# Padded score products, spread scans and row maxima split on GpSimd in a four-layer kernel

## The chip, the cores and the metric

The kernel runs on one core of a Trainium2 chip, as one launch. The metric is the device time of that core in microseconds: 1718.79 us as the median of three runs (1716.07 to 1720.85). An engine is named as the profile names it: PE is TensorE (matmuls), PEld its weight loads, DVE is VectorE, ACT is ScalarE, POOL is GpSimd, SP is SyncE, which issues the DMAs.

## The reference

The input is x of shape (4, 1024, 128), float32. Four layers follow one another, each as `x = x + layernorm(layer(layernorm(x)))`:

- a time-mixing layer: a recurrence over the 1024 positions with maxima and exponentials, then a feed-forward part of width 512,
- 16 gated experts of width 64 (4 of them chosen for each token) and a shared one,
- linear attention with 16 heads of 8: two decays for each head, and for every position a state that is multiplied by the decay and increased by key times value; the result is (query times state) / (query times summed keys),
- softmax attention and 8 experts (2 chosen). This last layer is the one that the change touches most:

```python
attn = jnp.einsum('bqhd,bkhd->bhqk', q, k) * scale
attn = jnp.where(causal, attn, -inf)
attn = jax.nn.softmax(attn, axis=-1)
out = jnp.einsum('bhqk,bkhd->bqhd', attn, v).reshape(B, S, C)
h = x + out @ wo.T
out = h + _moe(_rmsnorm(h, ffn_norm_w), gate_w, expert_w)
```

with S = 1024, 16 query heads of 8 dimensions, and 4 key heads, each used by 4 query heads.

## The kernel before

**Stages.** x is held transposed, 128 channels on the partitions, 512 positions (a half, `h`) in a tile. The time-mixing layer (`stage_a`) runs for three of the four batch items side by side. Then come the experts (`gates_b`, `stage_b`) with the linear attention of items 0 and 1 (`stage_c`) and the preparation of attention for item 0 (`heads`, `spread`). Up to here a scheduler orders the instructions of each engine. From `with tc.manual_schedule()` on, the order is the one in which the program issues them: this is the attention stage. It holds the attention of all four items, the linear attention of items 2 and 3, `heads` of items 1 to 3, and the last experts.

**Linear attention.** In `stage_c` the two states of a head and value dimension e are scans along the 512 positions on VectorE (`scan`, L620): one scan for each of two decays and nine e (eight value dimensions and the key sum), so 18 scans for a half. GpSimd makes key times value (`keyed`, L614) and adds the two states (`add`, L631), VectorE multiplies by the query (`times_q`, L637), TensorE sums over heads (`num_ps`, L674). Each bare `yield` ends a step.

**Attention.** float32 scores are made out of bfloat16 products: a query is split into three bfloat16 parts and so is a key, and the nine pairs of parts times eight dimensions are 72 contraction rows. Queries of a half lie in a tile `qr` of 128 partitions, 16 heads and 512 positions, keys in `keys_r`; `spread` fills rows 0 to 71 of both by DMA (L849, L853). Three more rows hold the row maximum, in three bfloat16 parts, against key rows that are -1: so the product of 75 rows (`KROWS` = 72, `ROWS` = 75) is the score less its maximum, and ScalarE takes the exponential straight from it.

For a block (b, i) of 128 queries there are two kinds of unit:

- `maxima(b, i)`: scores of 72 rows (`sm`; `late` at L874 for the half that the block lies in, with a causal mask added at L878, and `early` at L886 for the first half), and a maximum on VectorE for each (L882, L887). The last unit, `rows`, splits the maxima into three bfloat16 parts: five small VectorE instructions on 16 columns (L894 to L898; L894 only for blocks of the second half). The transpose on TensorE (`m_ps`, L901) is issued 9 ticks later, its copy (L905) 1 tick after that, and the three DMAs that place the rows in `qr` (L909) 3 ticks after that.
- `weighted(b, i)`: the 75-row product `sc` (L945), its exponential `pr` on ScalarE (L950), a causal select on GpSimd for the diagonal (L954), and, seven units later, the product with the values `av` (L937).

`units_of` interleaves the units of `weighted` for block n with those of `maxima` for block n + 2.

**Order in the attention stage.** After each unit the program calls `tick`. A tick issues what has come due, one step of `spread` if one is under way, and, by two accounts, steps of other work: `owed[0]` grows by `PER_TICK` = 0.5 and pays for one step of `front` (the linear attention and `heads` of the later items) whenever it has reached 1.0; `owed[1]` grows by 0.65 and pays for a step of the last experts (`experts`, `behind_it`). So the front advances one step in two ticks. Before block (b, 0) and block (b, 5) the program needs `heads` of (b, 1) and (b + 1, 0); if they are not ready, it calls `advance` until they are, with no unit in between:

```python
if i == 5 and b + 1 < NB:
    while (b + 1, 0) not in ready:
        advance()
```

Each engine takes its instructions in the order of issue, so an instruction that waits holds up those behind it on its engine.

Of the kernel before, what the change touches and what calls it, by code (L numbers as in the profile page):

```python
# [11 lines left out]
FP = mybir.dt.float32  # L12
BF = mybir.dt.bfloat16
AF = mybir.ActivationFunctionType
ALU = mybir.AluOpType
AX = mybir.AxisListType
PSUM = bass.MemoryType.PSUM

P = 128
NB = 4  # L20
T = 1024
CH = 512
NH = T // CH
# [16 lines left out]
def sandwich(ctx: ExitStack, tc: tile.TileContext, x, vecs, cmats, rope, wa, wb, wc, wd, out):  # L40
# [3 lines left out]
    nc = tc.nc  # L44
# [471 lines left out]
    rope3 = rope.rearrange("p (a t) -> p a t", a=2)  # L516

    LAG = 8

    def wait_for_it():  # L520
        for _ in range(LAG):
# [11 lines left out]
    def stage_c(b, pp, banks=None):  # L533
# [14 lines left out]
        for h in range(NH):  # L548
# [55 lines left out]
            q, k = phi  # L604
# [37 lines left out]
            for n, e in enumerate(order + [None, None, None]):  # L642

                if n + 1 < len(order):
                    keyed(order[n + 1])
                if e is not None:
                    scan(e, 0)
                    yield
                    scan(e, 1)
                    if 0 <= e < 5:  # L650
                        fetch(e + 3)
                yield
                if 1 <= n <= len(order):
                    add(order[n - 1])
                yield
                if 2 <= n <= len(order) + 1:
                    times_q(order[n - 2])
                yield
                if n == 3:
                    den = pp([P, CH], "den_ps")  # L660
                    parts = sums_e.pop(8)
                    for m, s_ in enumerate(parts):
                        nc.tensor.matmul(den, lhsT=selden, rhs=s_, start=(m == 0), stop=(m == len(parts) - 1))
                    yield
                    qz = pc.tile([P, CH], FP, tag="qz", name="qz", bufs=1)
                    nc.scalar.activation(qz, den, AF.Ln, bias=eps6)
                    nc.scalar.activation(qz, qz, AF.Exp, scale=-1.0)
                if n in ((7, 11) if banks is None else (6, 10)):
                    part = n // 8
                    pn = pp([P, CH], "num_ps")  # L670
                    four = [sums_e.pop(4 * part + e4) for e4 in range(4)]
                    for m in range(len(four[0])):
                        for e4 in range(4):
                            nc.tensor.matmul(  # L674
                                pn[32 * e4 : 32 * e4 + 32, :], lhsT=into[:, part, :], rhs=four[e4][m],
                                start=(m == 0), stop=(m == len(four[0]) - 1),
                            )
                    yield
                    o = pc.tile([P, CH], FP, tag="o", name="o")
                    nc.vector.tensor_mul(o, pn, qz)  # L680
                    os.append(o)
# [42 lines left out]
    while running or waiting:  # L724
        if waiting and (len(running) == 0 or (len(running) < SIDE and count >= BEHIND)):
            b = waiting.pop(0)
# [41 lines left out]

    KROWS, ROWS = 72, 75
    keys_r = [pk.tile([P, NH, 4, CH], BF, name=f"keys_r{i}") for i in range(2)]
    for kr in keys_r:
        nc.gpsimd.memset(kr[64:128], -1.0)

    def parts3(dst, src):

# [1 line left out]
        nc.gpsimd.tensor_copy(dst[:, 1], src)  # L779
        nc.gpsimd.tensor_sub(dst[:, 2], src, dst[:, 1])  # L780

    n3s, qrs, vas, drams, sums, pavs = {}, {}, {}, {}, {}, {}
    held = deque()
    behind_it = deque()
    moving = deque()


    now, due = [0], []
# [52 lines left out]
    def spread(b, h):  # L841

        dq, dk = drams[b]
        kr = keys_r[b % 2]
        qr = qrs[b, h] = pe.tile([P, 16, CH], BF, tag="qr", name="qr")
        for i in range(3):
            for j in range(3):
                rows = slice(3 * i + j, KROWS, 9)
                nc.sync.dma_start(  # L849
                    out=kr[rows, h].rearrange("r g t -> r (g t)"),  # L850
                    in_=dk[h, j].rearrange("(d g) t -> d (g t)", d=8),
                )
                nc.sync.dma_start(  # L853
                    out=qr[rows].rearrange("r h t -> r (h t)"),
                    in_=dq[h, i].rearrange("(d h) t -> d (h t)", d=8),
                )
                yield

    def maxima(b, i):


        qr, kr = qrs[b, i // 4], keys_r[b % 2]
        tb = slice(i % 4 * P, (i % 4 + 1) * P)
        half = i // 4
        n_s = (i % 4 + 1) * P
        in_bank = CH // n_s
        ms = pe.tile([P, 2, 16], FP, tag="ms", name="ms", bufs=3)

        def late(h0):
            sc = to_max([P, CH], "sm")  # L870
            view = r3(sc[:, : in_bank * n_s], in_bank)
            for k in range(in_bank):
                h = h0 + k
                nc.tensor.matmul(  # L874
                    view[:, k, :], lhsT=qr[0:KROWS, h, tb], rhs=kr[0:KROWS, half, h // 4, 0:n_s],
                    start=(k == 0), stop=False, skip_group_check=True,
                )
            nc.tensor.matmul(  # L878
                view[:, :, n_s - P :], lhsT=identb, rhs=later[:, :in_bank, :], start=False, stop=True,
                skip_group_check=True,  # L880
            )
            nc.vector.tensor_reduce(ms[:, 0, h0 : h0 + in_bank], view, AX.X, ALU.max)  # L882

        def early(h):
            sc = to_max([P, CH], "sm")
            nc.tensor.matmul(sc, lhsT=qr[0:KROWS, h, tb], rhs=kr[0:KROWS, 0, h // 4, :], start=True, stop=True)  # L886
            nc.vector.tensor_reduce(ms[:, 1, h : h + 1], sc, AX.X, ALU.max)  # L887

        def rows():
            mp = pe.tile([P, 3, 16], BF, tag="mp", name="mp", bufs=3)  # L890
            left = pe.tile([P, 16], FP, tag="ml", name="ml", bufs=3)
            top = ms[:, 0]
            if half:
                nc.vector.tensor_max(top, top, ms[:, 1])  # L894
            nc.vector.tensor_copy(mp[:, 0], top)
            nc.vector.tensor_sub(left, top, mp[:, 0])
            nc.vector.tensor_copy(mp[:, 1], left)
            nc.vector.tensor_sub(mp[:, 2], left, mp[:, 1])  # L898
            def turned():
                pm = to_max([48, P], "m_ps", BF)  # L900
                nc.tensor.transpose(pm, mp.rearrange("p i h -> p (i h)"), identb)  # L901

                def kept():
                    mt = pe.tile([48, P], BF, tag="mt", name="mt", bufs=3)
                    nc.vector.tensor_copy(mt, pm)  # L905

                    def placed():
                        for k in range(3):
                            nc.sync.dma_start(  # L909
                                out=qr[KROWS + k : KROWS + k + 1, :, tb], in_=mt[16 * k : 16 * k + 16, :]  # L910
                            )
                        placed_rows.add((b, i))

                    later_on(3, placed)

                later_on(1, kept)

            later_on(9, turned)

        units = [lambda h0=h0: late(h0) for h0 in range(0, 16, in_bank)]  # L920
        if half:
            units += [lambda h=h: early(h) for h in range(16)]
        return units + [rows]

    def weighted(b, i):


        qr, kr, va = qrs[b, i // 4], keys_r[b % 2], vas[b]
        tb = slice(i % 4 * P, (i % 4 + 1) * P)

        def products():
# [170 lines left out]
    def units_of(n):  # L1102

        first = weighted(*blocks[n])
        second = []
        if n + AHEAD < len(blocks):
            b, i = blocks[n + AHEAD]
            assert (b, i // 4) in qrs
            while moving:
                whole(moving.popleft())  # L1110
            second = maxima(b, i)
        done = 0
        for k, u in enumerate(first):
            yield u
            while done < len(second) and (done + 1) * len(first) <= (k + 1) * len(second):
                yield second[done]
                done += 1
        yield from second[done:]
# [13 lines left out]
    coming = front()  # L1132
    PER_TICK, PER_TICK_BEHIND = 0.5, 0.65
    owed = [0.0, 0.0]

    def advance():
        if next(coming, True):
            owed[0] = -1.0e9

    def tick():  # L1140
        now[0] += 1
        while due and min(due, key=lambda d: d[0])[0] <= now[0]:
            first = min(due, key=lambda d: d[0])
            due.remove(first)
            first[1]()
        if moving and next(moving[0], True):
            moving.popleft()
        owed[0] += PER_TICK
        if owed[0] >= 1.0:
            owed[0] -= 1.0  # L1150
            advance()
        owed[1] = min(owed[1] + PER_TICK_BEHIND, 1.5)
        if behind_it and owed[1] >= 1.0:
            owed[1] -= 1.0
            if next(behind_it[0], True):
                behind_it.popleft()
# [122 lines left out]
```

## Time and profile before

The profiled execution took 1715.55 us; its span from the first to the last instruction is 1713.8 us. The mean granted clock of TensorE is 0.85 of full speed. Where the stages lie, by the first and last records of their tiles:

| part | from, us | to, us |
|---|---|---|
| experts (`y_ps`) with linear attention of items 0 and 1 | 221 | 706 |
| scans of the linear attention, item 2, two halves | 826, 965 | 883, 1021 |
| scans of the linear attention, item 3, two halves | 1147, 1290 | 1216, 1356 |
| attention, first maximum of the manual order to last `sc` | 736 | 1659 |
| last experts after the attention | 1660 | 1714 |

The largest groups of the attention stage and those that the change touches:

| instruction | count | busy, us | mean, ns |
|---|---|---|---|
| ACT exponential `pr`, L950 | 576 | 328.2 | 595 |
| PE `sc`, 75 rows x 512, L945 | 576 | 234.1 | 422 |
| DVE maximum over 512, `early`, L887 | 256 | 165.0 | 682 |
| PE `sm`, 72 rows x 512, `early`, L886 | 256 | 99.6 | 417 |
| DVE scan with carried state, L620 | 32 | 49.8 | 1559 |
| POOL key times value, L614, attention stage | 35 | 48.6 | 1393 |

Busy times of one engine may be added up; those of different engines lie beside each other. [...]

### The profile page before, as it was taken

Reading aid. Unit: us, or ns where it says so; the run is one execution under the profiler, and the core shown is the slowest. Engines: PE = TensorE matmul, PEld = TensorE weight load, DVE = VectorE, ACT = ScalarE, POOL = GpSimd, SP = SyncE. Lnnn points to the kernel's source line nnn. Section 1 sums busy time; section 2 is a strip of 40 time slices with the busy share of each in tenths; the row PEclk is TensorE's granted clock in tenths of the full one; section 3 lists DMA queues with packets and bytes.
Section 4 is the critical chain, followed back from the end, with each engine's and each line's share of the span. In section 5 each row is a group of like instructions: output and inputs, shape, how many; then the busy total and the mean of one; then the engine's idle time right before and its main releaser. Section 6 shows DMA issues by size and latency. Waiting matters only on the chain.

```text
span 1713.8 us, 15167 instructions
## 1 busy us (share of the span) xinstructions
PE 1310.6 (76%) x4593; PEld 463.3 (27%) x4604; DVE 1168.9 (68%) x1991; ACT 856.7 (50%) x1565; POOL 655.9 (38%) x663
## 2 busy tenths in 40 slices
PE   2547887867865889678779869888887879889864
PEld 1213333312221323133223223322232223233311
DVE  4575676698775877867995597777779825577601
ACT  3457776624453457234436625645553345645561
POOL 5554353524252324323433363427227333122212
PEclk8669998978887999877779869987898669989996
DMA  2000110313033122101112111231113011110101
GB/s 97 13 7 6 25 50 25 96 40 108 13 111 110 53 65 85 44 12 34 45 58 70 53 57 54 70 92 46 38 37 101 21 48 64 45 61 29 54 22 56
DMA packets 59330, 90.49 MB, mean 53 GB/s; under 512 B 9904, under 2 KB 26800, under 8 KB 58544
## 3 DMA queue, kind: packets, MB, share of 16 engines
q1 hardware_dynamic: 59248, 89.52, 17.3%
q8 instruction: 36, 0.59, 0.1%
q14 instruction: 46, 0.38, 0.1%
HBM read 76.38 MB, written 12.71 MB: 52 GB/s over the span
## 4 chain that ended last, share of the span: by engine, by line
PE 32%; DVE 18%; ACT 6%; issue 4%; POOL 4%; DMA 2%; SPq 0%; POOLq 0%; DVEq 0%; ACTq 0%
PE av L937 8%; PE sc L945 5%; DVE ms L882 4%; DVE st L620 4%; ACT pr L950 3%; PE sm L874 3%; DVE ms L887 3%; PE y L1074 3%; PE sm L886 2%; PE ln_v L138 2%; PE num_ps L674 1%; POOL hid L473 1%; POOL share L1062 1%; PE sm L878 1%; PE g_ps L138 1%
## 5 line engine op out<-in xcount | busy, mean ns | idle before, releaser
L950 ACT ACTIVATE pr<-sc 128x512 f32<-128x512 f32 x576 | 328.2, 595 | 361.7 <-PE sc L945 358.0
L882 DVE TENSOR_REDUCE ms<-sm 128x1 f32<-128x512 f32 (+3 forms) x352 | 210.5, 633 | 114.2 <-PE sm L878 103.0
L945 PE MATMUL sc<-qr,keys_r 75*128 75x512 bf16 x576 | 234.1, 422 | 37.7 <-ACT pr L950 28.7
L887 DVE TENSOR_REDUCE ms<-sm 128x1 f32<-128x512 f32 x256 | 165.0, 682 | 56.4 <-PE sm L886 55.9
L937 PE MATMUL av<-pr,va 128*32 128x512 f32 x1152 | 183.1, 710 | 0.0
L954 POOL TENSOR_SCALAR_AFFINE_SELECT pr<-pr 128x512 f32<-128x512 f32 x128 | 89.4, 712 | 244.5 <-ACT pr L950 236.2
L874 PE MATMUL sm<-keys_r,qr 72*128 72x512 bf16 (+3 forms) x512 | 138.2, 337 | 46.3 <-DVE ms L882 43.9
L138 PE MATMUL ln_v<-rs,cm 128*128 128x512 f32 x176 | 113.0, 733 | 43.0 <-ACT rs L126 28.3
L473 POOL TENSOR_TENSOR hid<-hid,gate 128x512 f32<-128x512 f32 x64 | 81.9, 1280 | 162.9 <-DVE hid L468 124.6
L614 POOL TENSOR_TENSOR kv<-vrep,phi 128x512 f32<-128x512 f32 x64 | 85.6, 1342 | 115.0 <-issue 47.9
L1062 POOL TENSOR_TENSOR share<-n,every 128x512 f32<-128x512 f32 x64 | 87.2, 1373 | 91.1 <-DMA every<-row 70.5
L455 PE MATMUL y_ps<-hid,wbt 128*128 128x512 f32 x144 | 84.1, 669 | 46.3 <-DVE hid L474 44.4
L886 PE MATMUL sm<-keys_r,qr 72*128 72x512 bf16 x256 | 99.6, 417 | 25.0 <-DVE ms L887 20.6
L945 PEld LDWEIGHTS <-keys_r 75*128 75x128 bf16 x576 | 58.7, 106 | 153.2 <-issue 126.3
L878 PE MATMUL sm<-later,identb 128*128 128x128 bf16 (+2 forms) x341 | 90.5, 265 | 0.0
L474 DVE TENSOR_TENSOR hid<-hid,g 128x512 f32<-128x512 f32 x72 | 57.7, 801 | 46.7 <-POOL hid L473 39.9
L138 PE MATMUL u_ps<-n,wbt 128*128 128x512 f32 x144 | 77.3, 618 | 7.6 <-DVE hid L468 5.1
L138 PE MATMUL g_ps<-n,wbt 128*128 128x512 f32 x144 | 78.8, 630 | 3.7 <-DVE hid L463 1.6
L1074 PE MATMUL y<-share,wexp 128*128 128x512 f32 x128 | 70.8, 644 | 9.6 <-POOL share L1062 9.4
L874 PEld LDWEIGHTS <-qr 72*128 72x128 bf16 x512 | 51.0, 107 | 99.4 <-issue 82.8
L465 ACT ACTIVATE g<-hid 128x512 f32<-128x512 f32 x72 | 45.1, 626 | 55.4 <-DVE hid L463 55.3
L674 PE MATMUL num_ps<-st,cm 128*32 128x512 f32 x128 | 52.5, 777 | 25.7 <-DVE st L637 25.5
(300 smaller groups left out, 2394.9 us busy)
## 6 DMA issues: line engine op xcount, KB each, us to landing
gate<-rows SPq DMA_DIRECT2D x64, 256.0 KB
vrep<-v_rows SPq DMA_DIRECT2D x64, 256.0 KB
every<-row SPq DMA_DIRECT2D x64, 256.0 KB
qr<-dq SPq DMA_DIRECT2D x72, 128.0 KB
turn<-in_rope_dram SPq DMA_DIRECT2D x8, 512.0 KB
dq<-qp SPq DMA_DIRECT2D x8, 384.0 KB
keys_r<-dk SPq DMA_DIRECT2D x72, 32.0 KB
sums<-av_sb SPq DMA_DIRECT2D x128, 18.0 KB
```

Of the source, the lines that this page charges most:

```text
L138: nc.tensor.matmul(ps, lhsT=lhsT, rhs=rhs, start=True, stop=True)
L473: nc.gpsimd.tensor_mul(a, a, gate)
L874: nc.tensor.matmul(view[:, k, :], lhsT=qr[0:KROWS, h, tb], rhs=kr[0:KROWS, half, h // 4, 0:n_s], start=(k == 0), stop=False, skip_group_ch ...
L878: nc.tensor.matmul(view[:, :, n_s - P :], lhsT=identb, rhs=later[:, :in_bank, :], start=False, stop=True, skip_group_check=True,)
L882: nc.vector.tensor_reduce(ms[:, 0, h0 : h0 + in_bank], view, AX.X, ALU.max)
L886: nc.tensor.matmul(sc, lhsT=qr[0:KROWS, h, tb], rhs=kr[0:KROWS, 0, h // 4, :], start=True, stop=True)
L887: nc.vector.tensor_reduce(ms[:, 1, h : h + 1], sc, AX.X, ALU.max)
L937: nc.tensor.matmul(pavs[b, i][32 * g : 32 * g + 32, :], lhsT=va[:, j, g, :], rhs=pr, start=(j == 0), stop=(j == i),)
L945: nc.tensor.matmul(sc, lhsT=kr[0:ROWS, j // 4, g, j % 4 * P : (j % 4 + 1) * P], rhs=qr[0:ROWS, 4 * g : 4 * g + 4, tb], start=True, stop=True,)
L950: nc.scalar.activation(pr, sc, AF.Exp)
L1062: nc.gpsimd.tensor_mul(shares[-1], n4, gates[len(shares) - 1])
L1074: nc.tensor.matmul(y, lhsT=wexp[:, e, :], rhs=shares[e], start=False, stop=(e == 7))
```

## The change

- `KROWS` stays 72, a new `MROWS` is 125 and `ROWS` becomes 128. The queries get two fixed tiles `queries_r`, one for each half, in place of a rotating tag with two buffers of the same size; their rows 64 to 127 are set to zero once on GpSimd. The rows of the maxima move from 72 to 74 to rows 125 to 127. The products for the maxima now contract 125 rows, those for the weights 128; the rows between are zero in the queries and -1 in the keys.
- In `rows` the four splitting instructions go from VectorE to GpSimd. For blocks of the second half the maximum of the two parts, until now a `tensor_max` in place, becomes a `tensor_reduce` over pairs into a tile of its own, on VectorE.
- In the scan loop of `stage_c` the yields give the value `SCANS` = 1.25. `advance` takes the cost of the step just done from `owed[0]`, 0.75 for a plain step and 1.25 for one in the scan loop, and `tick` advances whenever the account is not negative. A forced `advance` is charged too.

```diff
+    STEP, SCANS = 0.75, 1.25
...
                 if e is not None:
                     scan(e, 0)
-                    yield
+                    yield SCANS
                     scan(e, 1)
                     if 0 <= e < 5:
                         fetch(e + 3)
-                yield
+                yield SCANS
                 if 1 <= n <= len(order):
                     add(order[n - 1])
-                yield
+                yield SCANS
                 if 2 <= n <= len(order) + 1:
                     times_q(order[n - 2])
-                yield
+                yield SCANS
...
-    KROWS, ROWS = 72, 75
+    KROWS, MROWS, ROWS = 72, P - 3, P
     keys_r = [pk.tile([P, NH, 4, CH], BF, name=f"keys_r{i}") for i in range(2)]
-    for kr in keys_r:
+    queries_r = [pe.tile([P, 16, CH], BF, tag=f"qr{i}", name=f"queries_r{i}", bufs=1) for i in range(NH)]
+    for kr, qr in zip(keys_r, queries_r):
         nc.gpsimd.memset(kr[64:128], -1.0)
+        nc.gpsimd.memset(qr[64:128], 0.0)
...
-                    view[:, k, :], lhsT=qr[0:KROWS, h, tb], rhs=kr[0:KROWS, half, h // 4, 0:n_s],
+                    view[:, k, :], lhsT=qr[0:MROWS, h, tb], rhs=kr[0:MROWS, half, h // 4, 0:n_s],
...
-            nc.tensor.matmul(sc, lhsT=qr[0:KROWS, h, tb], rhs=kr[0:KROWS, 0, h // 4, :], start=True, stop=True)
+            nc.tensor.matmul(sc, lhsT=qr[0:MROWS, h, tb], rhs=kr[0:MROWS, 0, h // 4, :], start=True, stop=True)
...
             if half:
-                nc.vector.tensor_max(top, top, ms[:, 1])
-            nc.vector.tensor_copy(mp[:, 0], top)
-            nc.vector.tensor_sub(left, top, mp[:, 0])
-            nc.vector.tensor_copy(mp[:, 1], left)
-            nc.vector.tensor_sub(mp[:, 2], left, mp[:, 1])
+                top = pe.tile([P, 16], FP, tag="top", name="top_ms", bufs=3)
+                nc.vector.tensor_reduce(top, ms.rearrange("p a h -> p h a"), AX.X, ALU.max)
+            nc.gpsimd.tensor_copy(mp[:, 0], top)
+            nc.gpsimd.tensor_sub(left, top, mp[:, 0])
+            nc.gpsimd.tensor_copy(mp[:, 1], left)
+            nc.gpsimd.tensor_sub(mp[:, 2], left, mp[:, 1])
...
-                                out=qr[KROWS + k : KROWS + k + 1, :, tb], in_=mt[16 * k : 16 * k + 16, :]
+                                out=qr[MROWS + k : MROWS + k + 1, :, tb], in_=mt[16 * k : 16 * k + 16, :]
...
     def advance():
-        if next(coming, True):
-            owed[0] = -1.0e9
+        step = next(coming, "end")
+        owed[0] -= 1.0e9 if step == "end" else step or STEP
...
         owed[0] += PER_TICK
-        if owed[0] >= 1.0:
-            owed[0] -= 1.0
+        if owed[0] >= 0.0:
             advance()
```

More of the change, by code (lines that the diff above doesn't have):

```diff
@@ L780, in parts3 @@
         nc.gpsimd.tensor_sub(dst[:, 2], src, dst[:, 1])
-    n3s, qrs, vas, drams, sums, pavs = {}, {}, {}, {}, {}, {}
+    n3s, vas, drams, sums, pavs = {}, {}, {}, {}, {}
     held = deque()
@@ L785, in sandwich @@
     moving = deque()
+    spreads = set()
     now, due = [0], []
@@ L844, in spread @@
         kr = keys_r[b % 2]
-        qr = qrs[b, h] = pe.tile([P, 16, CH], BF, tag="qr", name="qr")
+        spreads.add((b, h))
+        qr = queries_r[h]
         for i in range(3):
@@ L859, in maxima @@
     def maxima(b, i):
-        qr, kr = qrs[b, i // 4], keys_r[b % 2]
+        qr, kr = queries_r[i // 4], keys_r[b % 2]
         tb = slice(i % 4 * P, (i % 4 + 1) * P)
@@ L925, in weighted @@
     def weighted(b, i):
-        qr, kr, va = qrs[b, i // 4], keys_r[b % 2], vas[b]
+        qr, kr, va = queries_r[i // 4], keys_r[b % 2], vas[b]
         tb = slice(i % 4 * P, (i % 4 + 1) * P)
@@ L1107, in units_of @@
             b, i = blocks[n + AHEAD]
-            assert (b, i // 4) in qrs
+            assert (b, i // 4) in spreads
             while moving:
```

## The prediction

> **What bounds the kernel now.** I read the page first, then the busy time in stretches of the attention stage, then the clock's own periods, the groups by shape, and the chain of waits where the stage halts. The profiled execution took 1715.55 us (span 1713.8); the median of the three runs is 1718.79, 3.2 more, so the sum below is made against 1715.55 and 3.2 is added at its end.
>
> ```profile
> PE 1310.6 (76%) x4593; PEld 463.3 (27%) x4604; DVE 1168.9 (68%) x1991; ACT 856.7 (50%) x1565; POOL 655.9 (38%) x663
> ...
> PEclk8669998978887999877779869987898669989996
> ```
>
> No engine is full over the span, and TensorE's granted clock dips all along. The attention stage runs from about 735 to 1660 us. Counting the generators' yields gives 1219 ticks in it, one per unit. I cut it where the front's scans begin and end (their records on VectorE give the times):
>
> ```profile
> 823.00:903.00 80.00, 58.91 (x235) 18.05 (x235) 74.40 (x123) 30.95 (x72) 32.60 (x26) 0.72 0.20 60
> ...
> 964.00:1038.00 74.00, 58.69 (x273) 20.71 (x276) 66.53 (x95) 30.31 (x53) 34.26 (x30) 0.72 0.17 49
> ...
> 1146.00:1231.00 85.00, 71.98 (x314) 21.10 (x316) 67.61 (x75) 44.55 (x96) 50.09 (x40) 0.82 0.17 49
> ...
> 1292.00:1362.00 70.00, 53.68 (x193) 17.15 (x193) 62.80 (x84) 21.36 (x38) 44.12 (x31) 0.77 0.19 57
> 1362.00:1392.00 30.00, 19.69 (x47) 5.16 (x46) 8.78 (x18) 11.27 (x19) 7.78 (x11) 0.63 0.00 1
> ...
> 1422.00:1660.00 238.00, 206.11 (x1038) 70.35 (x1041) 129.88 (x262) 136.94 (x248) 62.15 (x72) 0.95 0.15 46
> ```
>
> Columns: stretch, length, busy us of PE, weight load, DVE, ACT, POOL, then granted clock. The first four are the scan stretches: 309 us for 376 ticks (0.82 a tick), VectorE busy 271.3 us of it (88%), clock 0.72 to 0.82. The last has no front: 384 ticks at 0.62, VectorE at 55%, clock 0.95. So **VectorE bounds the scan stretches**, TensorE the light ones; 1362 to 1392 is a halt.
>
> The clock deserves its own look. Its changes in the trace lie 3.41 us or multiples of that apart, and it is 0.50 or 1.00:
>
> ```profile
> 1192.90:1196.30 3.40, 3.36 (x12) 0.48 (x11) 3.16 (x5) 1.08 (x3) 3.40 (x5) 0.50 0.27 77
> 1196.30:1199.70 3.40, 3.19 (x12) 0.56 (x12) 3.40 (x3) 1.84 (x5) 1.89 (x2) 0.50 0.00 0
> 1199.70:1203.10 3.40, 3.14 (x12) 0.90 (x14) 3.36 (x5) 2.68 (x7) 1.26 (x1) 0.50 0.11 22
> ...
> 1209.90:1213.30 3.40, 2.93 (x23) 0.84 (x23) 0.47 (x1) 1.91 (x4) 0.88 (x1) 1.00 0.00 0
> ```
>
> TensorE is over 90% busy in the first three periods, and still the clock stays at half, while twice as many matmuls fit into the last.
>
> **Part 1, score products on all rows.** K goes from 75 to 128 (576 products, L945) and from 72 to 125 (768, L874 and L886). Duration: a 75x512 product takes 422 ns and a 128-row one of 512 columns (L878) 441 in the same mix, the weight loads 106 and 106, so the rows themselves cost nothing. The clock is the question. [...] I gave every matmul record its streaming time and weighted it by active rows x columns over 128 x 128: of 344 full-clock periods, "below 0.36 of full capacity means half clock next" misses 4; by busy time alone the best threshold misses 17. From half clock the same threshold (0.71 of a period) misses 21 of 149, busy time 32. With the padded rows put into the same records of the attention, 42% of the falls to half clock would be above the threshold, and of the half-clock periods 62% instead of 29%. So I take it that padded rows count. That zeros count like data no row shows, which is why it is rival A.
> Price: outside the scan stretches about 105 us run at half clock (2 x (1 - clock) x length of each stretch). Of the attention's 81 half-clock periods 51 have TensorE over 90% busy; these hold 3.6 ticks against 5.0 to 5.6 in busy full-clock ones, so a lifted one saves 30%. 105 x 0.63 x 0.7 x 0.3 = 14: **-15 us**, between 0 and -35.
>
> **Part 2, scans spread.** A plain step goes from 2 ticks to 1.5 (0.75 / 0.5), a scan step to 2.5. A half's scan loop has 45 scan steps and 3 plain ones: 96 ticks become 117; the four loops 376 (the last is cut short) become 468. The 92 extra ticks come out of light stretches, where they cost 92 x 0.62 = 57 us: 309 + 57 = 366 us now. After: VectorE has 271.3, less the row splitting in these stretches (22 us by its lines), plus 92 x 0.34 (129.9 / 384) = 31: 280 us; at the same 88% that is 318 us. **-48 us.** What is next: TensorE with 243 + 92 x 0.54 = 292 us even at the old clock, which is just under 318; so half of this could be lost (-24), and at the light pace everywhere 468 x 0.62 = 290 it would be -76.
> The halt at 1362: block (2,5) needs heads(3,0), and the front is forced on. Counting ticks, 40 steps are forced now and 26 after; the 14 fewer hold the end of the scans, o_ps, its norm and g_ps:
>
> ```profile
> 1367.27 1.99 PE o_ps L685 x4
> 1369.28 0.76 DVE hh L688
> ...
> 1373.96 2.09 PE g_ps L138 x2
> ...
> 1386.91 1.93 PE k_ps L821 x2
> ```
>
> 1367.27 to 1376.07 goes, 8.8 us, of which some 3 are TensorE work that has to stand elsewhere: **-6 us**.
> Against it: plain steps 25% closer. Per half of the linear attention 6 matmuls follow directly on an ACT or DVE result, per heads() 2: some 28 places, each with half to one tick (0.3 to 0.6 us) less lead. Hidden now by the lead, up to 17 us if none is left: **+8 us**.
>
> **Part 3, maxima split on GpSimd.**
>
> ```profile
> L896 DVE TENSOR_TENSOR ml<-ms,mp 128x16 f32<-128x16 f32 x32 | 13.7, 428 | 1.1
> L895 DVE CAST mp<-ms 128x16 bf16<-128x16 f32 x32 | 13.6, 426 | 0.9
> ...
> L898 DVE TENSOR_TENSOR mp<-ml,mp 128x16 bf16<-128x16 f32 x32 | 11.1, 346 | 1.1
> L897 DVE CAST mp<-ml 128x16 bf16<-128x16 f32 x32 | 9.9, 308 | 1.1
> L894 DVE TENSOR_TENSOR ms<-ms 128x16 f32<-128x16 f32 x16 | 9.8, 612 | 0.5
> ```
>
> 58.1 us leave VectorE; 16 reductions of 32 values come (nearest row L153, 186 ns: 3 us). 22 us of it are in Part 2's sum; of the other 33, where VectorE is 50 to 80% busy, I take a sixth: **-5 us**. [...] The rows say size decides: beside idle GpSimd each of these took 0.18 us (at 1366 us in the trace), beside busy GpSimd up to 1.2 (at 1194 us); GpSimd's own small copies (L206, one column) take 0.18, so the four are estimated at 0.2 to 0.3 each, 32 us on an engine 38% busy. The transpose that waits for them is queued 9 ticks (6 us) later: 0, and rival C if that lead is gone.
> Two memsets of 64x8192 come before the stage: the 64x4096 one took 3.51 us, so 2 x 7.0 on GpSimd at about 325 to 347 us, ahead of a hidden-gate product and u of the first linear attention, whose scans follow. The scheduler also redraws the order of the expert and linear-attention work from there to 735 us (same counts). Between -8 and +20: **+6 us**. The fixed query tiles use the same room and the same waits; 0.
>
> **Sum:** -15 - 48 - 6 + 8 - 5 + 6 = -60: 1715.6 - 60 + 3.2 = **1659 us**, own range 1630 to 1682.
>
> **Rivals.**
> A: zeros don't lift the clock. [...] Against: the threshold fits by the instruction's rows. TensorE at half clock then takes the place of VectorE in the scan stretches: -24 - 6 + 8 - 5 + 6 = -21: 1698 us (1682 to 1713).
> B: the scan stretches reach the light pace because warm TensorE and relieved VectorE help each other: -76 - 35 - 6 - 5 + 6 = -116: 1603 us. Against: the scans still run 1.5 us each on VectorE.
> C, slower: the splitting on GpSimd is late. Its queue is in order, and qs (L631) ahead of it waits for num_ps, once 8.05 us (1352 us), with two adds of 1.26 behind. That is more than 9 ticks; m_ps then blocks TensorE's queue and all units behind it. At 3 us for each of 32 blocks +96, net +36: 1755 us; it decides from 2 us a block. Against: few blocks meet such a wait.
> D: nothing measurable, the time returning in another wait: 1719 us.
>
> **How the numbers follow.** Forecast 0.57, A 0.17, B 0.11, C 0.10, D 0.05. About 0.3% (5 us) is what a measurement here tells from no change: faster 0.84, same 0.05, slower 0.11 (C and the outer edge of D). The range 1612 to 1714 takes the forecast, A and the near part of B, and leaves out C.
>
> **What would show it.** Clock in 823 to 1362 up from 0.77 to 0.88 or more, with few busy half-clock periods (A wrong); the scan loops below 0.72 us a tick; the halt near 1362 shorter by 6 to 9 us; the five row groups off VectorE; no TensorE wait on GpSimd before m_ps. Wrong if the clock stays, if TensorE waits for mp, or if the time before 735 us grows by over 20.

## The result, and the profile after

The changed kernel takes 1696.55 us (median of six runs, 1692.52 to 1702.43) against 1720.93 us for the kernel before in the same measurement: a ratio of 0.9862, with a 95% interval of 0.9836 to 0.9889. It is 24 us faster where 60 us were forecast. The profiled execution took 1702.43 us, with a span of 1700.7 and a mean granted clock of 0.878 (before: 0.850).

The page of the changed kernel, with the busy time of each engine and the granted clock in 40 slices:

```profile
PE 1279.2 (75%) x4592; PEld 460.1 (27%) x4604; DVE 1119.6 (66%) x1863; ACT 857.7 (50%) x1565; POOL 703.8 (41%) x793
...
PEclk8668898968798889968799989989998979989996
```

The 128 row splits have gone from VectorE (1991 instructions before, 1863 now) to GpSimd. TensorE does the same matmuls in 31 us less busy time, at a mean clock of 0.878 for 0.850: of the periods of 3.41 us, 369 are at the full clock in place of 344.

The same stretches as in the prediction, of the changed kernel: the four scan loops, the halt, and a stretch of the end that has no front (columns: stretch, length, busy us of PE, weight load, DVE, ACT, POOL, granted clock, DMA share, GB/s).

```profile
815.00:898.00 83.00, 58.90 (x273) 19.30 (x272) 75.82 (x125) 32.48 (x73) 40.53 (x41) 0.86 0.14 44
955.00:1033.00 78.00, 61.94 (x340) 20.94 (x341) 63.06 (x84) 41.06 (x73) 43.04 (x50) 0.93 0.18 50
1123.00:1220.00 97.00, 73.34 (x356) 23.50 (x352) 71.95 (x101) 50.32 (x108) 48.36 (x50) 0.91 0.16 45
1264.00:1353.00 89.00, 66.56 (x307) 24.52 (x307) 83.01 (x127) 32.13 (x58) 51.54 (x48) 0.87 0.17 51
1353.00:1375.00 22.00, 14.41 (x46) 4.58 (x42) 7.99 (x14) 11.89 (x22) 7.72 (x13) 0.84 0.00 1
...
1428.00:1645.00 217.00, 184.48 (x951) 63.04 (x953) 104.79 (x211) 126.70 (x230) 57.15 (x92) 0.96 0.15 42
```

Three things are to be seen. The clock in the scan loops has risen from 0.72-0.82 to 0.86-0.93. The loops hold 468 ticks in place of 376, and take about 348 us, where the prediction said 318. And VectorE is no longer near full in two of them: 63.06 of 78 and 71.95 of 97 us. So the resource that the prediction took for the bound of these stretches is not what sets the length of those two now; in the first and the last loop VectorE is still busy for 91% and 93%.

### The profile page after: what moved, and what is told of

It is laid out like the page before. It is cut to its first block, busy times and chain, and to the rows that moved or that the text cites. A ratio compares the mean times of both kernels' runs of the same rounds, so it can differ in the third digit from the quotient of the medians.

```text
span 1700.7 us, 15145 instructions
## 1 busy us (share of the span) xinstructions
PE 1279.2 (75%) x4592; PEld 460.1 (27%) x4604; DVE 1119.6 (66%) x1863; ACT 857.7 (50%) x1565; POOL 703.8 (41%) x793
## 5 line engine op out<-in xcount | busy, mean ns | idle before, releaser
L952 PE MATMUL sc<-queries_r,keys_r 128*128 128x512 bf16 x576 | 219.3, 396 | 43.1 <-ACT pr L957 32.4
L944 PE MATMUL av<-pr,va 128*32 128x512 f32 x1152 | 171.2, 656 | 2.1 <-POOL pr L961 2.1
L880 PE MATMUL sm<-keys_r,queries_r 125*128 125x512 bf16 (+3 forms) x512 | 132.8, 325 | 39.4 <-DVE ms L888 35.5
L892 PE MATMUL sm<-keys_r,queries_r 125*128 125x512 bf16 x256 | 94.1, 394 | 35.7 <-DVE ms L893 31.7
L1069 POOL TENSOR_TENSOR share<-n,every 128x512 f32<-128x512 f32 x64 | 83.6, 1319 | 73.7 <-DMA every<-row 44.1
L952 PEld LDWEIGHTS <-keys_r 128*128 128x128 bf16 x576 | 55.9, 101 | 151.3 <-issue 120.2
L474 DVE TENSOR_TENSOR hid<-hid,g 128x512 f32<-128x512 f32 x72 | 63.9, 889 | 42.5 <-POOL hid L473 35.6
L675 PE MATMUL num_ps<-st,cm 128*32 128x512 f32 x128 | 56.7, 883 | 29.3 <-DVE st L638 29.3
L880 PEld LDWEIGHTS <-queries_r 125*128 125x128 bf16 x512 | 50.0, 105 | 97.2 <-issue 80.8
```

What stands on the lines that cost most here:

```text
L880: nc.tensor.matmul(view[:, k, :], lhsT=qr[0:MROWS, h, tb], rhs=kr[0:MROWS, half, h // 4, 0:n_s], start=(k == 0), stop=False, skip_group_ch ...
L892: nc.tensor.matmul(sc, lhsT=qr[0:MROWS, h, tb], rhs=kr[0:MROWS, 0, h // 4, :], start=True, stop=True)
L944: nc.tensor.matmul(pavs[b, i][32 * g : 32 * g + 32, :], lhsT=va[:, j, g, :], rhs=pr, start=(j == 0), stop=(j == i),)
L952: nc.tensor.matmul(sc, lhsT=kr[0:ROWS, j // 4, g, j % 4 * P : (j % 4 + 1) * P], rhs=qr[0:ROWS, 4 * g : 4 * g + 4, tb], start=True, stop=True,)
L1069: nc.gpsimd.tensor_mul(shares[-1], n4, gates[len(shares) - 1])
```

## The experiments

The theory after the result was that the padding and the row splitting gain more than forecast and that the spacing of the front's steps loses. The rivals were that the spacing gains as forecast and the padding is worth nothing (rival A of the prediction), or that what was gained is taken back where GpSimd is late (rival C). Each ratio below is to the kernel before, run beside it on the same chip.

### Each part alone

`pad_only` is the change without its other two parts, and with the old account of ticks:

```diff
-    KROWS, ROWS = 72, 75
+    KROWS, MROWS, ROWS = 72, P - 3, P
```

> Only the padded products (fixed query tiles, two memsets, K 128 and 125), neither the spread scans nor the split on GpSimd. Theory (padded rows lift the clock, and the memsets with the redrawn order before the attention give part of it back): granted clock 0.87 to 0.885, half-clock periods of the attention well under the 81 of before, time 8 to 18 us under before. Rival (the clock is lifted but VectorE bounds the attention, so a warm TensorE only waits longer): clock 0.87 or more, time within 5 us of before.

`tiles_only` has the fixed query tiles and their memsets as well, but 72 and 75 rows:

```diff
-    KROWS, MROWS, ROWS = 72, P - 3, P
+    KROWS, MROWS, ROWS = 72, 72, 75
```

> The fixed query tiles and their two memsets, but products of 72 and 75 rows; scans and split as before. It prices the memsets and the order that the scheduler redraws before the attention. Theory: 4 to 12 us over before, all of it ahead of the first maxima of the attention (736 us before). Rival (the memsets are hidden): within 3 us of before.

`split_only` and `spread_only` are the kernel before with, in turn, the splitting on GpSimd and the new yields and account:

> Only the split of the row maxima on GpSimd. Theory (22 us of VectorE work leave the scan stretches, a third of it on the path, the rest hidden): 5 to 12 us under before. Rival (GpSimd's four instructions come late for the transpose or lengthen its adds and products for the scans): no faster than before, with TensorE waiting on GpSimd before m_ps.

> Only the spread scans: 75 and 72 rows and the query tiles as before, the split on VectorE. Theory (the scans' stretches are bound by VectorE and TensorE in turn, so thinning out VectorE's work alone is worth little while TensorE runs at half clock): 3 to 12 us under before, clock 0.84 to 0.86. Rival (the sum of the prediction, VectorE alone is the bound): 40 us or more under before. Second rival (the closer plain steps cost what the scans gain): within 3 us of before.

`no_spread` is the whole change with bare yields and the old account, that is padding and splitting together:

> The change without its spread scans: padded products and the split on GpSimd, the front at one step in two ticks. Theory (a scan holds up the attention once, about 1 us, however far the scans stand apart, so spreading them gained nothing and the closer plain steps cost about 20 us): the two gains add up, ratio to before 0.966 to 0.977 (1660 to 1680 us), faster than the whole change. Rival (the spread scans pay once the clock is up): ratio 0.986 or above, no faster than the whole change.

| version | median, us | ratio | 95% interval |
|---|---|---|---|
| `tiles_only` | 1718.61 | 1.0003 | 0.9969 to 1.0037 |
| `pad_only` | 1684.19 | 0.9807 | 0.9769 to 0.9845 |
| `split_only` | 1701.11 | 0.9908 | 0.9879 to 0.9937 |
| `spread_only` | 1738.12 | 1.0125 | 1.0078 to 1.0172 |
| `no_spread` | 1668.02 | 0.972 | 0.969 to 0.975 |

The padding is worth 1.9% (34 us) and the splitting 0.9% (17 us), both more than their expectations said. They add up: 0.9807 x 0.9908 = 0.9717, and 0.972 was measured for both, as expected. The spacing costs 1.25% by itself (20 us), which none of the three readings before the run allowed for, and beside the other two parts 28.5 us (1696.55 less 1668.02; by the two ratios 1.4%, 24 us). Tiles and memsets cost nothing that can be measured: the interval reaches from 5 us less to 6 us more. So the kernel without the third part is faster than the whole change.

The same stretches of `no_spread`, for comparison with the lines above:

```profile
817.00:891.00 74.00, 51.83 (x235) 16.79 (x234) 70.50 (x115) 31.03 (x72) 36.70 (x34) 0.86 0.20 59
951.00:1026.00 75.00, 53.82 (x273) 19.07 (x275) 66.10 (x83) 30.25 (x53) 43.89 (x42) 0.82 0.18 53
1128.00:1205.00 77.00, 62.71 (x315) 19.24 (x316) 56.44 (x63) 43.66 (x95) 55.44 (x52) 0.98 0.16 51
1261.00:1331.00 70.00, 49.90 (x211) 15.62 (x209) 65.33 (x85) 23.71 (x42) 48.17 (x38) 0.90 0.20 61
1331.00:1356.00 25.00, 14.54 (x33) 4.39 (x31) 5.10 (x12) 9.07 (x15) 6.11 (x10) 0.73 0.00 1
...
1386.00:1618.00 232.00, 198.12 (x1028) 68.14 (x1030) 113.41 (x226) 135.69 (x246) 67.69 (x106) 0.98 0.15 47
```

Set against these, each scan loop of the changed kernel is longer, by 9, 3, 20 and 19 us, and holds more matmuls of the attention. To see whether that is a gain, time has to be set against ticks. I assigned every tick the start of the unit before it (the records of `sc` and of the maxima carry the order), and cut the attention by the program's own steps (where a loop is taken to end moves its sum by a few us):

| part of the attention | before | `spread_only` | `no_spread` | changed kernel |
|---|---|---|---|---|
| scan loops, us / ticks | 312 / 376 | 367 / 468 | 295 / 376 | 348 / 468 |
| other stretches with front, us / ticks | 349 / 458 | 331 / 381 | 324 / 458 | 314 / 381 |
| halt, us / ticks | 26 / 0 | 24 / 15 | 24 / 0 | 23 / 15 |
| after the front's end, us / ticks | 237 / 384 | 225 / 354 | 232 / 384 | 218 / 354 |

A tick without front takes 0.61 us here. From `no_spread` to the changed kernel the scan loops take 53 us more and hold 92 ticks more, worth 56: a gain of 3, no more than the cuts are sure to. The other stretches take 10 us less but have lost 77 ticks, worth 47: a loss of 37. The halt gains 2 and holds 15 ticks worth 9: a gain of 11. The end loses 4. The sum, a loss of 27, is the difference of the two spans (1700.7 and 1673.7). In loss (+) and gain (-), from before to `spread_only` the same sum is -1 in the scans, +29 in the other stretches, -11 at the halt and +7 at the end.

### Other spacings

In the changed kernel, with other prices for a plain and a scan step:

```diff
-    STEP, SCANS = 0.75, 1.25
+    STEP, SCANS = 1.0, 0.75
```

and 1.2 with 0.5, and 1.0 with 1.0.

> The whole change, but the spacing turned round: a plain step costs 1.0 (2 ticks), a scan step 0.75 (1.5 ticks), so the scans stand closer than before and no step has to be forced. Theory (fixed price for each scan): as fast as the run without spread scans or up to 10 us faster, since the forced halt of about 29 us near block (2,5) is gone: 1655 to 1675 us. Rival (VectorE's load in the scan stretches is the bound, so closer scans cost): 10 us or more slower than the run without spread scans.

> The extreme: plain step 1.2 (2.4 ticks), scan step 0.5 (1 tick), so a scan loop takes about 51 ticks in place of 117; one forced step. Theory (fixed price for each scan, plain steps better far apart): within 8 us of the run with 1.0 and 0.75, scan loops at well over 1 us a tick, all other stretches at 0.60 to 0.65. Rival (VectorE's load bounds): 63 us for each of four loops, some 30 to 50 us slower than the run without spread scans.

> The whole change with both costs 1.0: the spacing of before (2 ticks for every step) under the new account, in which forced steps are charged (the last heads of item 3 come 78 ticks later). It tells the account's effect from the spacing's. Theory: within 5 us of the run without spread scans. Rival (charging the forced steps is what costs): 10 us or more slower than that run.

| version | ticks a scan step | median, us | ratio | 95% interval |
|---|---|---|---|---|
| `s120_050` | 1 | 1700.71 | 0.9893 | 0.9864 to 0.9921 |
| `s100_075` | 1.5 | 1691.57 | 0.9836 | 0.9805 to 0.9868 |
| `s100_100` | 2 | 1700.71 | 0.9889 | 0.9859 to 0.9919 |
| changed kernel | 2.5 | 1696.55 | 0.9862 | 0.9836 to 0.9889 |

No spacing comes near `no_spread`. `s100_075` and `s120_050` are 24 and 33 us slower than it, as their rivals had said and not as the theory had (the second only just); but the new account puts their plain steps on other ticks as well, so the time alone does not tell why. The traces say more about Part 2. Over the light pace of 0.605 us a tick, a scan loop costs, for each of its 72 scans, about 1.7 us with steps 1 tick apart, 1.3 with 1.5, 0.94 with 2 (`no_spread`) and 0.90 with 2.5. Two loops of `s120_050` show the crowded end:

```profile
827.00:889.00 62.00, 38.13 (x133) 10.41 (x132) 57.58 (x67) 19.73 (x48) 34.05 (x28) 0.70 0.17 55
...
1263.00:1330.00 67.00, 39.06 (x165) 13.86 (x164) 61.12 (x89) 17.82 (x33) 42.51 (x37) 0.75 0.18 58
```

VectorE is nearly full there (57.58 of 62, 61.12 of 67 us), the clock is at 0.70 and 0.75, and few attention matmuls pass: 133 and 165 matmuls in all, where the first and the last loop of `no_spread` hold 235 and 211. So spreading does work as the prediction meant it, but it has paid off by 2 ticks, where the kernel already stood. A scan with carried state takes VectorE 1.56 us in the kernel before and 1.51 in the changed one: that it stands further from the next does not make it much shorter.

That `s100_100` loses 33 us against `no_spread` was not expected: its steps are 2 ticks apart too. It differs in two things only. The new account lets a step go at once, where the old one waits until a full step has been earned, so the whole front runs two ticks earlier; and forced steps are charged.

### The place of the front's steps

Each of these changes one of the two:

```diff
-    owed = [0.0, 0.0]
+    owed = [-1.0, 0.0]
```

in `s100_100` is `acct_even`: the ticks of `no_spread`, with forced steps charged. Starts of 1.0, 0.5 and -1.0 in `no_spread`, with its old account, are `early_one` (front 2 ticks earlier), `odd_ticks` (1 earlier) and `late_one` (2 later).

> The run with both costs 1.0, with the account started at -1.0: then every step of the front falls on the same tick as in the run without spread scans until block (2,5), and only the charge for the forced steps is left (the last heads of item 3 come 78 ticks later). Theory (the place of the front's steps among the units is what cost 33 us, the charge little): 1668 to 1678 us. Rival (the charge costs): 1690 us or more.

> The run without spread scans (old account, forced steps free), with the account started at 1.0: the front is one step, 2 ticks, ahead all the way, as it was with both costs 1.0. Theory (the place of the steps costs): 1685 to 1698 us, some 20 to 27 us over the run without spread scans for a shift of two ticks. Rival (the charge or the account's form costs): within 5 us of 1668.

> The run without spread scans, the account started at 0.5: every step of the front one tick earlier, on odd ticks. If the place among the units matters, the time moves by 5 to 25 us, and no theory here says which way; if it does not, within 4 us of 1668.

> The run without spread scans, account started at -1.0: the front one step (2 ticks) later all the way, so 42 steps have to be forced near block (2,5) in place of 40. If the place matters in both directions, 1675 to 1695 us; if the start of before was not special and only an early front costs, 1664 to 1674 us.

`spread_free` is the whole change with forced steps not charged; `spread_m05`, `spread_m10` and `spread_m15` are the whole change with the account starting at -0.5, -1.0 and -1.5.

> The whole change, but forced steps are not charged, as before: the last heads of item 3 follow at once. Theory (late heads cost about 5 us by the stretch after block (2,5)): 2 to 8 us faster than the whole change, 1689 to 1695 us. Rival (the charge is most of what the spread scans cost): 1675 us or less.

> The whole change with its account started at -0.5, so that all steps of the front shift by a tick or less. If the spacing itself is worth nothing and only the place of the steps decides, the whole change at other starts spreads over the same 1668 to 1695 us that shifts of the unspread front gave, and at least one of three starts falls under 1686. If the spacing itself costs (its closer plain steps), all three stay at 1690 us or more.

> The whole change with its account started at -1.0: the second of three starts; the same two readings as for -0.5.

> The whole change with its account started at -1.5: the third of three starts; the same two readings as for -0.5.

| version | front | median, us | ratio | 95% interval |
|---|---|---|---|---|
| `late_one` | unspread, 2 ticks later | 1668.98 | 0.9719 | 0.9684 to 0.9753 |
| `no_spread` | unspread | 1668.02 | 0.972 | 0.969 to 0.975 |
| `odd_ticks` | unspread, 1 earlier | 1685.6 | 0.9794 | 0.9769 to 0.982 |
| `early_one` | unspread, 2 earlier | 1692.75 | 0.9861 | 0.9832 to 0.989 |
| `acct_even` | unspread, charged | 1676.66 | 0.9744 | 0.9717 to 0.9771 |
| `spread_free` | spread, not charged | 1692.16 | 0.9847 | 0.9815 to 0.9879 |
| `spread_m05` | spread | 1695.62 | 0.9876 | 0.9838 to 0.9914 |
| `spread_m10` | spread | 1687.01 | 0.9826 | 0.979 to 0.9861 |
| `spread_m15` | spread | 1688.26 | 0.9828 | 0.9788 to 0.9868 |

A shift of the whole front by one or two ticks, with nothing else changed, costs 0.7 to 1.4%. The upper end is as much as the whole of Part 2. Charging the forced steps costs less: the intervals of `acct_even` and `no_spread` overlap, and so do those of `spread_free` and the changed kernel. The two together, 24.7 us (`early_one`) and 8.6 (`acct_even`), make up the 33 us of `s100_100`. The spread front at four starts lies between 1687 and 1697 us, never near 1668. The unspread one lies between 1668 and 1693, so the two ranges overlap. The three shifted starts met neither of the two readings set down for them (one under 1686, or all at 1690 or more), and how much of the 28 us is the closer spacing of plain steps and how much their place is **not settled** by these runs.

Where a shift costs can be seen by laying the traces tick over tick. In ticks 74 to 290 `s100_100` needs 171 us where `no_spread` needs 158. First `no_spread`:

```profile
792.70:951.10 158.40, 128.24 (x591) 44.17 (x592) 119.99 (x198) 86.91 (x172) 64.23 (x73) 0.94 0.20 60
```

and `s100_100`:

```profile
793.60:964.70 171.10, 135.65 (x591) 45.43 (x592) 122.76 (x199) 86.87 (x171) 63.99 (x72) 0.89 0.16 51
```

The same 591 matmuls need 7.4 us more of TensorE at a clock of 0.89 for 0.94, and TensorE also idles about 5 us more. Two places of `early_one`, which has the same shift, tell how. Its chain of waits near 865 us (start, duration, what):

```profile
864.03 1.30 POOL qs L631
865.33 1.23 POOL num L998
...
866.60 2.09 PE wo_ps L1003 x2
```

GpSimd does the linear attention's `add` (qs) first and the attention's `num` after it, as they were issued, and `wo_ps` on TensorE (866.60 us) waits for `num` (865.33 us, 1.23 us long), with all score products behind it. The `add` itself stood waiting for TensorE's `num_ps`, with GpSimd idle for 6.18 us. First `early_one`, then `no_spread`, where `num` goes 6.7 us ahead of that `add` (868.73 us):

```profile
864.01 1.31 POOL L631 TENSOR_TENSOR qs<-st,st 128x512 f32<-128x512 f32 x1 [6.18 <-PE num_ps L674]
...
862.03 1.73 POOL L998 TENSOR_TENSOR num<-num,den 128x512 f32<-128x512 f32 x1
```

In `no_spread` the same `wo_ps` takes 1.02 us in place of 2.09 and does not stand in the chain, which runs over VectorE there; `early_one` loses about 5 us in these 32 ticks (180 to 212). The second place is the start of the next half. In `early_one`:

```profile
933.16 1.82 PE qk_ps L138 x2
```

In `no_spread`:

```profile
926.69 0.86 PE qk_ps L138 x2
```

The same matmul pair takes 1.82 us in `early_one` in place of 0.86, as at half clock: in the trace of the kernel before, successive records of this form (512 columns, float32) start 429 ns apart at a clock of 1.00 and 853 at 0.50. A pause came before: in one period of the clock TensorE was busy for only 1.59 of 3.40 us and waited for the exponentials of ScalarE, which was busy for 3.37; the next period was at a clock of 0.51. The same happened once more from 927.8 to 934.6 us: eight `av` took 1.86 us at 931.30, where eight took 0.99 at 938.59.

```profile
921.00:924.40 3.40, 1.59 (x11) 0.35 (x10) 1.46 (x3) 3.37 (x8) 0.00 (x0) 1.00 0.11 22
924.40:927.80 3.40, 3.40 (x8) 1.33 (x5) 0.00 (x0) 0.39 (x1) 0.00 (x0) 0.51 0.02 4
```

Ticks 250 to 270 cost another 6 us.

The changed kernel has such a place at the very start of the attention. The front's first `ln_v` on TensorE gets its input from ScalarE at 751 us in both kernels (750.76 in `no_spread`, 751.16 in the changed one). In `no_spread` it is issued behind six units, in the changed kernel behind three, because its plain steps follow each other faster and the first goes at once. So the fourth unit of `no_spread` starts right after the last `o_ps` (743.0 us), and that of the changed kernel 12 us after it (742.5 us). First `no_spread`, then the changed kernel:

```profile
743.46 0.39 PE L879 MATMUL sm<-keys_r,queries_r 125*128 125x128 bf16 x4
...
754.89 0.63 PE L880 MATMUL sm<-keys_r,queries_r 125*128 125x128 bf16 x4
```

Counted from that `o_ps`, tick 80 is reached after 51.9 us in `no_spread`, 65.9 in the changed kernel and 60.0 in `spread_m15`, whose first `ln_v` stands behind six units again. So of 14 us some 6 went back with a later start, and 8 stayed; these may be the closeness of the plain steps or the place of the others.

### The wait for `num`

The trace of `no_spread` has one wait that the kernel before hardly has: TensorE's `wo_ps` for GpSimd's `num` (columns: us in total, times, longest).

```profile
PE wo_ps L1003 <- POOL num L998: 9.3, 5, 2.5
```

In the kernel before it is 2.7 us in total, in `split_only` 10.4, in `pad_only` 3.9. So it comes with the splitting, which puts 128 more instructions into GpSimd's queue. In the changed kernel:

```profile
PE wo_ps L1004 <- POOL num L999: 13.1, 5, 4.6
```

`num_dve` is `no_spread` with that product on VectorE:

```diff
-                    nc.gpsimd.tensor_mul(num, num, den)
+                    nc.vector.tensor_mul(num, num, den)
```

> The run without spread scans (padded rows, split on GpSimd), with the product before the output projection of the attention (num times den, 8 of 128x512) moved from GpSimd to VectorE. With the split on GpSimd TensorE's wait of wo_ps for that product rose from 2.7 us (before) to 9.3 us inside the attention. If that wait is on the path: 3 to 8 us under 1668, wo_ps waiting less than 4 us. If it only stood in front of another wait: within 3 us of 1668.

It takes 1661.39 us, 0.9668 of the kernel before (0.9622 to 0.9714). Its wait:

```profile
PE wo_ps L1003 <- DVE num L998: 2.1, 3, 1.3
```

Most of the wait is gone, and the time is 6.6 us below that of `no_spread`, about what was waited and within what was expected; as the two intervals still overlap a little, the gain is likely but not shown. This is the lowest median of all versions: 2.0% below the changed kernel (0.9668 / 0.9862) and 3.3% below the one before.

## Why the prediction was wrong

The sign was right; the size was not. The parts forecast at -20 together (padding -15, splitting -5) gave about 50, and the part forecast at -46 (-48 - 6 + 8) lost 20 to 28. That the measured time lies inside the wide range of 1612 to 1714 us (though not in the forecast's own, 1630 to 1682) is luck: two errors of opposite sign met.

**Part 2 is the step that failed**, in two of its terms. The first is "at the same 88% that is 318 us. **-48 us.**" It treated a scan loop as a load of VectorE that is filled to a constant share, so that ticks brought in from elsewhere would fill the gaps. Measured, the loops took 348 us. VectorE's load there was near the estimate (293.8 us against 280) but its share fell to 85%. The cost over the light pace belongs to the scan, not to the tick: 1.11 us for each of 72 scans before (over its own light pace of 0.617), 0.94 in `no_spread`, 0.90 after. 92 ticks brought in cost nearly what they cost elsewhere: 53 us from `no_spread`, 55 from before to `spread_only`, where 57 had been reckoned. The rate of 0.82 us a tick, from which the prediction started, mixed the two.

The second is "+8 us" for plain steps set closer, bounded at 17. It was +29 alone and +37 beside the other parts. The bound counted 28 waits of one tick each and put the attention's own waits at nothing: where the front's steps fall between the units decides who is ahead in GpSimd's and TensorE's queues, and with that whether TensorE pauses and then runs at half clock, as in `early_one` (busy for 1.59 of 3.40 us, then at 0.51). That run shows that this alone can be worth 24 us; how much of the +37 it is stays open. The prediction noted that "half to one tick" of lead would go; it did not note that the new account also moves every step of the front to another tick.

Of the signs named beforehand, the clock did rise as asked for: 0.92 over 815 to 1353 us. (The 0.77 from which the prediction started is near the mean of its four scan lines; the whole stretch from 823 to 1362 us was at 0.83.) But the scan loops stayed above 0.72 us a tick (348 / 468 = 0.74). The halt, forecast at -6, went from 30 to 22 us in the windows, and gained 11 with its 15 ticks counted: the order of the steps at its end came out as forecast.

**Part 1** had the right mechanism and too small a size: -15 was forecast, -34 measured. Rival A is refuted, although its 1698 us is close to the measured time: zeros counted here. `pad_only` and `tiles_only` differ in the row counts alone, and their clocks are 0.874 and 0.841. The 0.36 of full capacity is a line fitted to the records of the trace of before; the streaming time of a product can be read there from the starts of successive ones (for 512 bfloat16 columns 0.22 us at full clock and 0.43 at half, for a float32 record of 512 columns 0.43 and 0.85). With the padded rows counted as rows, the same line still sorts the clock's periods of the changed kernel: it misses 7 of 369 full-clock ones and 12 of 120 half-clock ones. (There, with nearly all rows in use, busy time alone sorts them as well: at its own best lines streaming time without the weight misses 6 and 6. What tells the two apart is the gain of `pad_only`.) The half-clock periods of the attention fell from 81 to under 50 in `pad_only`, and those with TensorE over 90% busy from 51 to 20. In two lines of `pad_only`, a scan loop that was at 0.72 before and one that was at 0.82:

```profile
829.00:906.00 77.00, 53.12 (x235) 16.69 (x235) 74.03 (x123) 30.95 (x72) 32.22 (x26) 0.80 0.19 58
...
1145.00:1221.00 76.00, 61.81 (x313) 18.82 (x314) 67.10 (x74) 43.59 (x95) 50.65 (x40) 0.98 0.17 51
```

The mis-sized term is "outside the scan stretches about 105 us run at half clock": it priced the padding outside these stretches alone, on the ground that VectorE bounds the inside, where by the same formula the four scan lines of the prediction hold another 149 us at half clock. By ticks, from before to `pad_only`, the other stretches with front gave 10 us and the part after the front's end 7, about the -15 of the forecast; another 15 came from inside the scan loops, although VectorE was busy for 74.03 of 77 us in the first of them. A share near 90% on one engine did not exclude a gain through another.

**Part 3** was forecast at -5, with another 22 us of VectorE's load counted inside Part 2, and gave -17 by itself. By ticks, from before to `split_only`, 11 us came from the scan loops and 18 from the other stretches with front, and 8 were lost after the front's end; so the "sixth" of 33 us was the term too small. The operations on GpSimd cost about what was estimated, 35.5 us in all against 32. Two of their six rows of the changed kernel (the means of the six go from 217 to 410 ns):

```profile
L904 POOL CAST mp<-ml 128x16 bf16<-128x16 f32 x32 | 10.5, 329 | 2.1
...
L905 POOL TENSOR_TENSOR mp<-ml,mp 128x16 bf16<-128x16 f32 x32 | 7.9, 247 | 2.6
```

The reduction on VectorE took 184 ns, as its neighbour row had said. Half of the 128 operations are casts with one input (220 to 410 ns on GpSimd, 308 and 426 on VectorE before), the other half have two (217 to 247 ns on GpSimd, 346 and 428 on VectorE before). Rival C did not happen: the trace of the changed kernel has no wait of `m_ps` for GpSimd. Its mechanism did, on a smaller scale and at another place, `wo_ps` waiting for `num` (13.1 us in all, 2.7 before).

**Memsets and the redrawn order** were put at +6, and `tiles_only` came out at 1.0003; its interval ends at 1.0037, so the +6 is at its very edge.

Still open: how the loss of Part 2 divides between spacing and place, and why the front may come 2 ticks later for nothing (`late_one`) but not 1 or 2 earlier. In the profiled executions the attention of `early_one` is 21 us longer than that of `no_spread`; the two places shown make about 11 of them. Another 5 lie before tick 80, of which the first `ln_v`, issued two units earlier here too, is a part; the cause of the rest is not known.

## What to carry to other kernels

Before work is moved from a light stretch into a crowded one, split the crowded stretch's time into a part that goes with the inserted work and a part that goes with the host: if the excess belongs to the inserted work, as here, moving ticks gains little or nothing (3 us for 92 ticks from `no_spread` to the changed kernel). In an order written by hand, a change of spacing is also a change of place, and a shift of one or two slots can be worth as much as the change itself (17 and 24 us here); so run the unshifted order beside two or three shifted ones before a verdict on the spacing. Where several parts come in one change, run each alone: here two parts gained 50 us and the third took half of it back.

## What was not expected of the hardware

- Rows in which one operand is zero and the other -1 raised the granted clock (0.874 in `pad_only`, 0.841 in `tiles_only`), and the product paid no time for them: the shortest `sc` takes 375 ns with 128 rows and 376 with 75, the median 379 in both. The mean fell from 422 to 396 ns in the changed kernel, as more of them ran at full clock.

```profile
L952 PE MATMUL sc<-queries_r,keys_r 128*128 128x512 bf16 x576 | 219.3, 396 | 43.1 <-ACT pr L957 32.4
```

- Small instructions of 16 columns took GpSimd no longer than VectorE in this mix: the profile of the changed kernel has 35.5 us for the 128, that of the kernel before 48.3 on VectorE (the four rows of the prediction, 308 to 428 ns each).
- The place of the front's steps came out as time by way of the clock: ticks 74 to 290, with the same matmuls, took 158 us at a clock of 0.94 in `no_spread` and 171 us at 0.89 in `s100_100`; 7.4 us of the difference is TensorE's longer busy time.
